# Attention values in four 32-column tiles, softmax sums as separate products, roots on ScalarE, in a planned GNN kernel

## Chip, cores and metric

One core of a Trainium2 chip. The metric is device microseconds of one execution. The profile is of one execution of the same program.

## The reference, cut to what matters

The kernel computes two layers on 16 graphs of 1024 nodes with 256 features. The first layer is masked attention with 8 heads of 32 columns:

```python
e = jnp.einsum('whqd,whkd->whqk', q, k)
e = jnp.where(e >= 0, e, ALPHA * e)
attn = jax.nn.softmax(jnp.where(adj[:, None] > 0, e, NEG), axis=-1)
h = jnp.einsum('whqk,whkd->whqd', attn, v)
out = _layernorm(h.transpose(0, 2, 1, 3).reshape(w, n, H * DH), g1, b1)
out = jnp.concatenate([out, features], axis=-1) @ Wffn.T
x = _layernorm(out, g2, b2) + features
```

The second layer applies two graph attentions (scores are a sum of a row term and a column term, softmax over the masked graph, then a product with the node rows), adds the residual, normalizes, and runs a feed-forward net of 256 to 1024 to 256 columns with a second residual and normalization. All is float32.

## The kernel before

The work of one graph is called a batch; `b` counts them. A head's 1024 x 1024 scores are made transposed, keys on partitions, in 8 tiles `t` of 128 keys by 1024 queries. Each tile goes through a chain of four engines:

- `all_scores` (L601): TensorE, two matmuls of 512 columns into a PSUM tile `ps_s` (two such tiles).
- `weights`: ScalarE multiplies by 0.2 (L619), VectorE takes the larger of that and the score (L621), ScalarE takes the exponential (L624), GpSimd multiplies by the mask (L628). The result is `p`, one of 5 buffers.
- `all_values` (L650): TensorE multiplies by `v`. The 33 columns of a head are 32 values and one column of -1, so that row 33 of the result is the softmax sum. The two halves of the queries go to rows 0 and 64 of one PSUM bank `ps_a`, as two column tiles of the array.
- `after_head`: the bank is copied out (`ho`), transposed (L677), and the values are divided by the sum (L682, L684).

The products of values are issued in pairs of tiles:

```python
for t in range(d, d + GV):
    p = probs.pop((b, h, t))
    for nh in range(NH):
        m = VW if t else 64
        nc.tensor.matmul(acc[nh * 64:nh * 64 + m, :], v[:, t, c:c + m],
                         p[:, nh * HALF:(nh + 1) * HALF], start=(t == 0), stop=(t == NT - 1))
```

`project` makes the transposed features, queries, keys and values of the next batch (L475, L507), and `make_mask` turns its adjacency into 8-bit masks (L412, L422). `rest` does all that follows the attention of the batch before: `rows_pair`, the two graph attentions (`attend` on VectorE, L838 and L841; products L876 and L901), `normed_pair`, and the feed-forward net (L941, L969). So TensorE always has work of two batches at hand. `stats` computes a normalization's mean and variance on VectorE, and the reciprocal root on GpSimd as an addition (L338) and a power (L340).

The order of instructions on every engine is written by a planner at build time. `Order` runs each function above as a thread. A thread announces an operation with its cost (`on`), waits for events, takes and gives buffers, and has an aim, a due time that is a share of a batch's length `SLOT` (the tables `AIM` and `EARLY`). The planner keeps a clock for each engine, adds a hand-over time `HOP` between engines, treats the operations marked `shared` on VectorE and GpSimd as exclusive, and among the operations that could begin within `WINDOW` ns emits the one due first. The chip then runs each engine's list in that order; the waits between engines are semaphores that the framework adds. DMAs are issued from SP (`qk_halves`, `qs`, `ks`, `x_kept`, the outputs) and from ScalarE (`adj_i`, `xr`).

PSUM buffers for all other products (`ps_m`, taken with `misc`) are a ring of three.

Of the kernel before, what the change touches and what calls it, by code (L numbers as in the profile page):

```python
# [18 lines left out]
EPS = 1e-5  # L19
H = 8  # L20
P = 128
# [13 lines left out]
class Order:  # L35
# [5 lines left out]

    HOP = dict(PE=100.0, ACT=70.0, DVE=60.0, POOL=70.0, SP=60.0)
    WINDOW = 300.0

# [3 lines left out]
    def __init__(self, **pools):  # L54
        self.clock = defaultdict(float)
        self.port = 0.0
        self.transfers = 0.0
        self.stretch, self.done, self.half = 0, 0.0, True
        self.pools = {k: [0.0] * n for k, n in pools.items()}
        self.queues = defaultdict(list)  # L60
        self.events = {}
        self.waiting = defaultdict(list)
        self.active = []
        self.made = 0
        self.now = 0.0
        self.busy = defaultdict(float)

    def add(self, thread, aim, ready=0.0):
        self.made += 1
        self.step({"gen": thread, "aim": aim, "no": self.made, "ready": ready}, None)  # L70

    def step(self, th, sent):
        while True:
# [19 lines left out]
            elif what == "take":  # L93
# [3 lines left out]
                th["ready"] = max(th["ready"], self.pools[arg].pop(0))  # L97
            elif what == "give":
                queue = self.queues[arg]
                if queue:  # L100
                    other = min(queue, key=lambda o: (o["aim"], o["no"]))
                    queue.remove(other)
                    other["ready"] = max(other["ready"], th["ready"])
                    self.step(other, None)
                else:
                    self.pools[arg].append(th["ready"])
                    self.pools[arg].sort()
# [26 lines left out]
    def run(self):  # L134
        while self.active:
            could = []
            for th in self.active:
                costs, shared, delay = th["op"]
                best = None
                for engine, cost in costs.items():  # L140
                    ready = th["ready"]
                    if th.get("last", ())[:2] == (engine, ready):
                        ready -= self.HOP[engine]
                    t = max(self.clock[engine], ready)
                    if shared and engine in ("DVE", "POOL"):
                        t = max(t, self.port)
                    if best is None or t + cost < best[0] + best[2]:
                        best = t, engine, cost
                could.append((best, th))
            first = min(c[0][0] for c in could)  # L150
            (t, engine, cost), th = min((c for c in could if c[0][0] <= first + self.WINDOW),
                                        key=lambda c: (c[1]["aim"], c[1]["no"]))
            if th["op"][1] and engine in ("DVE", "POOL"):

                lead = 100.0 if engine == "DVE" else -100.0
                before = [c for c in could if c[1]["op"][1] and c[0][1] in ("DVE", "POOL")
                          and c[0][1] != engine and c[0][0] + lead < t]
                if before:
                    (t, engine, cost), th = min(before, key=lambda c: (c[1]["aim"], c[1]["no"]))
            costs, shared, delay = th["op"]  # L160
            self.active.remove(th)
            end = self.clock[engine] = self.end(engine, t, cost)
# [4 lines left out]
            th["ready"] = end + self.HOP[engine]  # L167
# [10 lines left out]
def on(shared=False, delay=0.0, **costs):  # L178
    return "on", (costs, shared, delay)
# [45 lines left out]
def unshifted_path(  # L225
# [19 lines left out]
    VW = DH + 1  # L245
    GV = 2
    YW = D + 2
# [6 lines left out]
    AIM = dict(mask0=0.759, x=0.818, x_step=0, mask=0.747, mask_step=0.0264, qk0=0.614, qk1=0.898,  # L254
               qk_step=0.0231, v0=0.832, v1=0.974, v_step=0.0591, rows=-0.244, rows_step=0.0408, first0=0.12,
               first1=0.252, graph0=-0.009, graph1=0.21, graph_step=0, second=0.355, second_step=0.0335,
               normed=0.78, normed_step=0.026, ff_wait=(None, 0, 1, 0), ff=(0.532, -0.011, 0.487, 0.497),
               ff_step=0.0386, fast0=0.425, fast1=0.938, fast15=0.832, lead=3.15)

    EARLY = dict(x=0.87, x_step=0.005, mask=0.747, mask_step=0.0296, qk0=0.692, qk1=0.909, qk_step=0.0345,  # L260
                 v0=0.774, v1=1.001, v_step=0.0568, rows=-0.139, rows_step=0.0071, first0=0.082, first1=-0.169,
                 graph0=-0.195, graph1=-0.027, graph_step=0, second=0.302, second_step=0.0335, normed=0.781,
                 normed_step=0.02, ff_wait=(None, 0, 1, 0), ff=(0.633, -0.001, 0.488, 0.497), ff_step=0.0386)
# [6 lines left out]
    bufs = dict(misc=3, scores=2, acc=1, p=5, stacks=2, stage=2, adj=2, adjb=2, pair=18,  # L270
# [6 lines left out]
    def misc(dtype=FT):  # L277
        return psum.tile([P, HALF], dtype, tag="misc", name="ps_m", bufs=bufs["misc"])
# [9 lines left out]
    minus_half = const.tile([P, TPH], FT, name="minus_half")  # L288
    nc.gpsimd.memset(minus_half, -0.5)
# [25 lines left out]
    def evacuate(n):  # L315
        return on(DVE=140 + 1.06 * n, ACT=150 + 0.87 * n)

    def evacuate_by(n):

        return on(DVE=190 + 1.06 * n, ACT=250 + 0.87 * n)  # L320
# [5 lines left out]
    def stats(srcs):  # L326
# [3 lines left out]
        for i, src in enumerate(srcs):  # L330
            st = small.tile([P, 6], FT, name="st")
            yield on(DVE=420)
            nc.vector.bn_stats(st, src)
            yield on(DVE=185)
            nc.vector.bn_aggr(mv[:, i, :], st)  # L335
        rs = small.tile([P, n], FT, name=f"rs{n}")
        yield on(POOL=260)
        nc.gpsimd.tensor_scalar(rs, mv[:, :, 1], EPS, None, op0=OP.add)  # L338
        yield on(POOL=450 + 150 * n, shared=True)
        nc.gpsimd.tensor_tensor(rs, rs, minus_half[:, :n], op=OP.pow)  # L340
        return mv, rs

    def normalized(dst, srcs, mv, rs):
        for i, (row, src) in enumerate(zip(dst, srcs)):
            if row is src:
                yield on(DVE=340, shared=True)
            else:
                yield on(DVE=440)
# [38 lines left out]
    def mask_part(b, t, halves):  # L387
# [22 lines left out]
        for i, ai in enumerate(ints):  # L410
            yield on(DVE=440, shared=True)
# [8 lines left out]
        yield on(PE=90 + 112 * n)  # L420
# [3 lines left out]
        yield on(ACT=150 + 225 * n)  # L424
# [19 lines left out]
    def x_pair(b, u):  # L444
# [7 lines left out]
        yield on(PE=450)  # L452
# [7 lines left out]
    def qk_part(b, g, o, nh):  # L460
# [12 lines left out]
        yield on(PE=1720)  # L473
# [3 lines left out]
        yield on(ACT=590)  # L477
        nc.scalar.copy(high.bitcast(FR), pa)
        yield on(DVE=690)
# [20 lines left out]
    def v_part(b, g, u):  # L500
# [3 lines left out]
        yield on(PE=1000)  # L504
# [6 lines left out]
        dst = vs[b, g][:, 2 * u:2 * u + 2, :G * VW].rearrange("p t (h c) -> p t h c", c=VW)[:, :, :, :DH]  # L511
        src = pa[:, :2 * P].rearrange("p (t h c) -> p t h c", t=2, c=DH)
# [7 lines left out]
    def project_v(b, g, t0):  # L520
        yield take("v")
        v = buf([P, NT, G * VW + 31], "v", "v")
        vs[b, g] = v
        yield on(POOL=500)
        nc.gpsimd.memset(v[:, :, G * VW:], 0.0)
        nc.gpsimd.memset(v[:, :, :G * VW].rearrange("p t (h c) -> p t h c", c=VW)[:, :, :, DH:], -1.0)
# [3 lines left out]
    def warm_up():  # L530
# [3 lines left out]
        nc.scalar.copy(small.tile([P, TPH], FT, name="warm", bufs=1), minus_half)  # L534
# [46 lines left out]
    def all_scores():  # L581
        for b in range(B):
# [4 lines left out]
            for h in range(H):  # L587
                yield wait(("stack", b, h))
                q, kk = stacks[b, h]
                n = 2 if b else 1  # L590
                for t in range(0, NT, n):
                    due = t0 + (h * NT + t) / 2 * pace(b)
                    yield aim(due, AIM["lead"] * PACE)
                    for _ in range(n):
                        yield take("scores")
                    ps = [psum.tile([P, N], FT, tag="scores", name="ps_s") for _ in range(n)]
                    yield on(PE=450 * n)
                    for i in range(n):
                        for nh in range(NH):
                            cols = slice(nh * HALF, (nh + 1) * HALF)  # L600
                            nc.tensor.matmul(ps[i][:, cols], kk[:, (t + i) * P:(t + i + 1) * P], q[:, cols],  # L601
                                             start=True, stop=True)
                    if t + n == NT:
                        yield give("stacks")
                    for i in range(n):
                        yield start(weights(b, h, t + i, ps[i]), due + i * PACE / 2)

    def weights(b, h, t, ps):
# [3 lines left out]
        if b == 0:  # L612
            engine = yield on(ACT=1050, DVE=1230)
        else:
            engine = yield on(ACT=1050)
# [4 lines left out]
        yield on(DVE=1220)  # L620
        nc.vector.tensor_tensor(p, p, ps, op=OP.max)  # L621
        yield give("scores")
        yield on(ACT=1080)
# [3 lines left out]
        yield on(POOL=2050, shared=True)  # L627
# [3 lines left out]
    def all_values():  # L631
        for b in range(B):
            for h in range(H):
                g, c = h // G, (h % G) * VW
# [4 lines left out]
                acc = psum.tile([P, HALF], FT, tag="acc", name="ps_a", bufs=bufs["acc"])  # L639
                for d in range(0, NT, GV):  # L640
                    for t in range(d, d + GV):
                        yield wait(("p", b, h, t))
                    yield aim(begin[b] + (h * NT + d + 2) / 2 * pace(b), SLOT)
                    yield on(PE=240 + 860 * GV)
                    for t in range(d, d + GV):
                        p = probs.pop((b, h, t))
                        for nh in range(NH):

                            m = VW if t else 64
                            nc.tensor.matmul(acc[nh * 64:nh * 64 + m, :], v[:, t, c:c + m],  # L650
                                             p[:, nh * HALF:(nh + 1) * HALF],
                                             start=(t == 0), stop=(t == NT - 1))
                    for t in range(GV):
                        yield give("p")
                yield start(after_head(b, h, acc), begin[b] + (h + 1) * NT // 2 * pace(b))
                if h % G == G - 1:
                    yield give("v")
            yield start(rest(b), work.now)

    def after_head(b, h, acc):  # L660
# [6 lines left out]
        used = 64 + VW  # L667
# [7 lines left out]
        yield on(PE=450)  # L675
        for i in range(TPH):
            nc.tensor.transpose(pt[:, i * P:i * P + used], ho[:used, i * P:(i + 1) * P], ident[:used, :used])  # L677
        yield give("pair")
        src = pt.rearrange("p (i j c) -> p j i c", i=TPH, j=NH)
# [766 lines left out]
```

## Time and profile before

| What | Value |
|---|---|
| Runs shown, median of 3 | 4487.69 us (4481.99 to 4490.15) |
| Profiled execution, first to last instruction | 4479.9 us |
| TensorE matmuls, busy | 4325.9 us, 20299 records |
| TensorE weight loads, busy | 2866.3 us |
| VectorE busy | 3311.9 us |
| ScalarE busy | 2887.7 us |
| GpSimd busy | 2474.9 us |
| Mean granted TensorE clock | 0.990 |

Of the profiled execution the page gives the span alone, so its time is the span; the median of the runs is 7.8 us above it, 0.2%. A record of a matmul has a modelled end, so its mean duration holds the time that its results take to come out; how long it keeps the array is seen from the distance of two starts. A float32 matmul leaves two records. An engine's idle time is put down to what ended it, not to what was slow.

### The profile page before, as it was taken

Reading aid. Unit: us, or ns where it says so; the run is one execution under the profiler, and the core shown is the slowest. Engines: PE = TensorE matmul, PEld = TensorE weight load, DVE = VectorE, ACT = ScalarE, POOL = GpSimd, SP = SyncE. Lnnn points to the kernel's source line nnn. Section 1 sums busy time; section 2 is a strip of 40 time slices with the busy share of each in tenths; the row PEclk is TensorE's granted clock in tenths of the full one; section 3 lists DMA queues with packets and bytes.
Section 4 is the critical chain, followed back from the end, with each engine's and each line's share of the span. In section 5 each row is a group of like instructions: output and inputs, shape, how many; then the busy total and the mean of one; then the engine's idle time right before and its main releaser. Section 6 shows DMA issues by size and latency. Waiting matters only on the chain.

```text
span 4479.9 us, 57088 instructions
## 1 busy us (share of the span) xinstructions
PE 4325.9 (97%) x20299; PEld 2866.3 (64%) x20299; DVE 3311.9 (74%) x5263; ACT 2887.7 (64%) x4015; POOL 2474.9 (55%) x1544
## 2 busy tenths in 40 slices
PE   8888999999999999999999999999999999999998
PEld 3444656667666675766667666676666667666587
DVE  6877867687776877778777776877778777776754
ACT  6666675666667666666666666666666666666631
POOL 5756565554565556556554565546556554665610
PEclk9989999999999999999999999999999999999999
DMA  6423222232232313223231232323223231232100
GB/s 187 114 66 87 66 73 77 73 92 73 68 88 63 107 59 86 76 59 99 64 106 55 74 96 62 103 63 80 80 64 99 64 102 55 71 92 55 27 22 20
DMA packets 156209, 343.57 MB, mean 77 GB/s; under 512 B 21751, under 2 KB 24333, under 8 KB 155917
## 3 DMA queue, kind: packets, MB, share of 16 engines
q1 hardware_dynamic: 112140, 260.13, 20.8%
q10 hardware_dynamic: 43776, 79.71, 6.1%
q8 instruction: 164, 2.69, 0.3%
q14 instruction: 129, 1.05, 0.1%
HBM read 239.09 MB, written 100.66 MB: 76 GB/s over the span
## 4 chain that ended last, share of the span: by engine, by line
PE 69%; DVE 18%; issue 5%; POOL 5%; ACT 2%; DMA 0%; POOLq 0%; ACTq 0%; DVEq 0%
PE ps_a L650 16%; PE ps_s L601 9%; PE ps_m L901 8%; PE ps_m L876 8%; PE ps_m L941 7%; PE ps_m L969 6%; DVE att L841 5%; DVE att L838 5%; POOL p L628 4%; DVE p L621 4%; PE ps_m L785 3%; PE ps_m L475 3%; PE ps_m L753 2%; PE ps_m L756 2%; PE ps_m L355 2%
## 5 line engine op out<-in xcount | busy, mean ns | idle before, releaser
L628 POOL TENSOR_TENSOR p<-p,mask 128x1024 f32<-128x1024 f32 x1024 | 2232.2, 2197 | 1564.6 <-ACT p L624 1444.7
L621 DVE TENSOR_TENSOR p<-p,ps_s 128x1024 f32<-128x1024 f32 x1024 | 1211.1, 1214 | 399.3 <-ACT p L619 397.8
L624 ACT ACTIVATE p<-p 128x1024 f32<-128x1024 f32 x1024 | 1080.9, 1058 | 377.5 <-DVE p L621 355.7
L619 ACT ACTIVATE p<-ps_s 128x1024 f32<-128x1024 f32 x995 | 974.9, 1025 | 186.7 <-PE ps_s L601 172.1
L650 PE MATMUL ps_a<-p,v 128*33 128x512 f32 (+1 forms) x4096 | 1000.6, 606 | 24.2 <-POOL p L628 22.9
L601 PE MATMUL ps_s<-qs,ks 128*128 128x512 f32 x2048 | 634.5, 428 | 39.2 <-DVE p L621 38.3
L601 PEld LDWEIGHTS ps_s<-qs,ks 128*128 128x128 f32 x2048 | 349.5, 190 | 343.2 <-DVE p L621 106.2
L650 PEld LDWEIGHTS ps_a<-p,v 128*33 128x33 f32 (+1 forms) x4096 | 199.7, 114 | 531.3 <-issue 405.3
L901 PE MATMUL ps_m<-y,att 128*128 128x256 f32 x2048 | 480.5, 380 | 12.7 <-ACT v L516 11.0
L941 PE MATMUL ps_m<-rT,wf 128*128 128x256 f32 x2048 | 479.8, 384 | 10.7 <-ACT z L313 3.6
L969 PE MATMUL ps_m<-wf,hid 128*128 128x256 f32 x2048 | 475.1, 381 | 10.6 <-ACT xT L313 8.9
L876 PE MATMUL ps_m<-y,att 128*128 128x258 f32 x2048 | 472.4, 381 | 0.0
L969 PEld LDWEIGHTS ps_m<-wf,hid 128*128 128x128 f32 x2048 | 379.4, 190 | 78.6 <-issue 14.8
L876 PEld LDWEIGHTS ps_m<-y,att 128*128 128x128 f32 x2048 | 385.2, 189 | 63.6 <-issue 3.3
L901 PEld LDWEIGHTS ps_m<-y,att 128*128 128x128 f32 x2048 | 375.0, 189 | 77.3 <-ACT v L516 13.1
L941 PEld LDWEIGHTS ps_m<-rT,wf 128*128 128x128 f32 x2048 | 380.9, 192 | 63.4 <-ACT z L313 3.8
L838 DVE SCALAR_TENSOR_TENSOR att<-first,second 128x1024 f32<-128x1024 f32 x256 | 354.4, 1384 | 73.2 <-ACT first L825 73.2
L841 DVE SCALAR_TENSOR_TENSOR att<-mask,att 128x1024 f32<-128x1024 fp8e4 x256 | 352.0, 1375 | 8.7
L846 ACT ACTIVATE y<-y,check 128x258 f32<-128x258 f32 x256 | 130.9, 511 | 305.3 <-DVE check L844 278.4
L338 POOL TENSOR_SCALAR rs<-mv 128x2 f32<-128x2 f32 (+1 forms) x224 | 60.0, 268 | 410.9 <-DVE mv L335 410.8
L412 DVE TENSOR_SCALAR adj_b<-adj_i 128x512 fp8e4<-128x512 int32 x256 | 234.0, 958 | 14.8 <-DMA adj_i<-in_adj_dram 9.3
L950 ACT ACTIVATE hid<-ps_m,columns 128x256 f32<-128x256 f32 x372 | 159.2, 472 | 119.8 <-PE ps_m L941 94.3
(105 smaller groups left out, 4232.5 us busy)
## 6 DMA issues: line engine op xcount, KB each, us to landing
qs<-qk_halves SPq DMA_DIRECT2D x256, 256.0 KB, 4.2
ks<-qk_halves SPq DMA_DIRECT2D x256, 256.0 KB, 5.1
adj_i<-in_adj_dram ACTq DMA_DIRECT2D x240, 256.0 KB, 3.5
qk_halves<-high SPq DMA_DIRECT2D x128, 256.0 KB, 2.4
qk_halves<-low SPq DMA_DIRECT2D x128, 256.0 KB, 3.6
xr<-in_x_dram ACTq DMA_DIRECT2D x64, 256.0 KB, 3.1
x_kept<-x SPq DMA_DIRECT2D x64, 256.0 KB, 4.8
x<-x_kept SPq DMA_DIRECT2D x64, 256.0 KB, 6.8
```

Source lines behind the costliest of these rows:

```text
L601: nc.tensor.matmul(ps[i][:, cols], kk[:, (t + i) * P:(t + i + 1) * P], q[:, cols], start=True, stop=True)
L619: nc.scalar.activation(p, ps, AF.Copy, scale=ALPHA)
L621: nc.vector.tensor_tensor(p, p, ps, op=OP.max)
L624: nc.scalar.activation(p, p, AF.Exp)
L628: nc.gpsimd.tensor_tensor(p, p, mask_of(b, t), op=OP.mult)
L650: nc.tensor.matmul(acc[nh * 64:nh * 64 + m, :], v[:, t, c:c + m], p[:, nh * HALF:(nh + 1) * HALF], start=(t == 0), stop=(t == NT - 1))
L838: nc.vector.scalar_tensor_tensor(e, first[:, 0, :], second[:, j:j + 1], first[:, 1, :], op0=OP.mult, op1=OP.max)
L841: nc.vector.scalar_tensor_tensor(e, mask_of(b, j), -1.0, e, op0=OP.mult, op1=OP.mult, accum_out=sums[:, j:j + 1])
L876: nc.tensor.matmul(pa[:, cols:cols + width], big[:, j, i * P:(i + 1) * P], rows[:, j, :width], start=(j == 0), stop=(j == NT - 1))
L901: nc.tensor.matmul(pa[:, i * D:(i + 1) * D], big[:, j, t * P:(t + 1) * P], y2[:, j, :D], start=(j == 0), stop=False)
L941: nc.tensor.matmul(pa[:, i * 2 * P:(i + 1) * 2 * P], wf1[:, dc, hc * P:(hc + 1) * P], rT[:, dc, :], start=(dc == 0), stop=(dc == DC - 1))
L969: nc.tensor.matmul(pa[:, i * D:(i + 1) * D], hid[hc // 2][:, hc % 2, i * P:(i + 1) * P], wf2[:, hc, :], start=(hc == 0), stop=False)
```

## The change

- `v` has no columns of -1. A tile's values are four matmuls of 32 columns by 256 queries, each to its own 32 rows of the bank's first half. The sums are four matmuls of the same shape with a constant block of -1 as weights, to the bank's second half.
- Of a head's four pairs of tiles, the first two are added on VectorE (`add_pair`), and the sum product is taken of the added tile, behind the values of the next pair. The last two pairs have a sum product for each tile. `p` has 6 buffers.
- The transposes of `after_head` cover all 128 rows.
- `stats` takes the root on ScalarE: a logarithm, then an exponential of -0.5 times it. The activation table is loaded by name at the start.
- Scores are planned one tile at a time in every batch.
- The planner has new costs for most operations, a hand-over before (`HOP`) and after (`TAIL`) an operation, a cost `SWITCH` for TensorE's change between tiled and whole-array products, another rule for the order of `shared` operations, and new due times. The three `ps_m` buffers have a tag each, and a product takes the one that the planner chose.

```diff
-    HOP = dict(PE=100.0, ACT=70.0, DVE=60.0, POOL=70.0, SP=60.0)
+    HOP = dict(PE=53.0, ACT=35.0, DVE=36.0, POOL=80.0, SP=60.0)
+    TAIL = dict(PE=163.0, ACT=103.0, DVE=84.0, POOL=42.0, SP=0.0)
     WINDOW = 300.0
+    SWITCH = 93.0
...
-                lead = 100.0 if engine == "DVE" else -100.0
                 before = [c for c in could if c[1]["op"][1] and c[0][1] in ("DVE", "POOL")
-                          and c[0][1] != engine and c[0][0] + lead < t]
+                          and c[0][1] != engine and c[0][3] < asked]
...
+            if engine == "PE":
+                if narrow != self.narrow:
+                    cost += self.SWITCH
+                self.narrow = narrow
...
-    bufs = dict(misc=3, scores=2, acc=1, p=5, stacks=2, stage=2, adj=2, adjb=2, pair=18,
+    bufs = dict(misc=3, scores=2, acc=1, p=6, stacks=2, stage=2, adj=2, adjb=2, pair=18,
...
-        return psum.tile([P, HALF], dtype, tag="misc", name="ps_m", bufs=bufs["misc"])
+        return psum.tile([P, HALF], dtype, tag=f"misc{work.slot['misc']}", name="ps_m", bufs=1)
...
+    minus_ones = const.tile([P, DH], FT, name="minus_ones")
+    nc.gpsimd.memset(minus_ones, -1.0)
...
         rs = small.tile([P, n], FT, name=f"rs{n}")
-        yield on(POOL=260)
-        nc.gpsimd.tensor_scalar(rs, mv[:, :, 1], EPS, None, op0=OP.add)
-        yield on(POOL=450 + 150 * n, shared=True)
-        nc.gpsimd.tensor_tensor(rs, rs, minus_half[:, :n], op=OP.pow)
+        yield on(ACT=98)
+        nc.scalar.activation(rs, mv[:, :, 1], AF.Ln, bias=eps)
+        yield on(ACT=98)
+        nc.scalar.activation(rs, rs, AF.Exp, scale=-0.5)
...
-        v = buf([P, NT, G * VW + 31], "v", "v")
-        vs[b, g] = v
-        yield on(POOL=500)
-        nc.gpsimd.memset(v[:, :, G * VW:], 0.0)
-        nc.gpsimd.memset(v[:, :, :G * VW].rearrange("p t (h c) -> p t h c", c=VW)[:, :, :, DH:], -1.0)
+        vs[b, g] = buf([P, NT, G * DH], "v", "v")
...
-                n = 2 if b else 1
-                for t in range(0, NT, n):
+                for t in range(NT):
...
+                def product(w, p, at, first, last):
+                    for i in range(4):
+                        nc.tensor.matmul(acc[i * DH:(i + 1) * DH, at:at + QN], w, p[:, i * QN:(i + 1) * QN],
+                                         start=first, stop=last)
+
+                added = []
                 for d in range(0, NT, GV):
+                    last, adds = d + GV == NT, d < ADDED * GV
                     for t in range(d, d + GV):
                         yield wait(("p", b, h, t))
+                    if added:
+                        yield wait(("p added", b, h, d - GV))
                     yield aim(begin[b] + (h * NT + d + 2) / 2 * pace(b), SLOT)
-                    yield on(PE=240 + 860 * GV)
...
+                    ps = [probs.pop((b, h, t)) for t in range(d, d + GV)]
+                    for t, p in zip(range(d, d + GV), ps):
+                        yield on(PE=430, narrow=True)
+                        product(v[:, t, c:c + DH], p, 0, t == 0, False)
+                        yield aim(begin[b], BIG)
+                    if adds:
+                        yield start(add_pair(b, h, d, ps), begin[b] + (h * NT + d + 2) / 2 * pace(b))
+                    for p in added if adds else added + ps:
+                        yield on(PE=430, narrow=True)
+                        product(minus_ones, p, QN, False, last and p is ps[-1])
                         yield give("p")
+                    added = ps[:1] if adds else []
...
+    def add_pair(b, h, d, ps):
+        yield on(DVE=1180, shared=True)
+        nc.vector.tensor_tensor(ps[0], ps[0], ps[1], op=OP.add)
+        yield give("p")
+        yield fire(("p added", b, h, d))
...
-            nc.tensor.transpose(pt[:, i * P:i * P + used], ho[:used, i * P:(i + 1) * P], ident[:used, :used])
+            nc.tensor.transpose(pt[:, i * P:(i + 1) * P], ho[:, i * P:(i + 1) * P], ident)
```

Nearly every other `on(...)` has a new cost in the same manner, and every entry of `AIM` and `EARLY` that the batches use is changed.

## Prediction

> **What bounds the kernel now.** I read the busy table first, then the groups of instructions, then the timeline of one stretch of TensorE, then the table of stages, and last the waits of the weight loads.
>
> ```profile
> PE 4325.9 (97%) x20299; PEld 2866.3 (64%) x20299; DVE 3311.9 (74%) x5263; ACT 2887.7 (64%) x4015; POOL 2474.9 (55%) x1544
> ```
>
> TensorE is busy for 97% of the span, the next engine (VectorE) for 74%. A busy PE is not yet a PE at its peak, so the groups and the timeline must show what its time is made of.
>
> ```profile
> L628 POOL TENSOR_TENSOR p<-p,mask 128x1024 f32<-128x1024 f32 x1024 | 2232.2, 2197 | 1564.6 <-ACT p L624 1444.7 <-issue 72.6 <-PE ps_m L941 11.7
> L621 DVE TENSOR_TENSOR p<-p,ps_s 128x1024 f32<-128x1024 f32 x1024 | 1211.1, 1214 | 399.3 <-ACT p L619 397.8
> L650 PE MATMUL ps_a<-p,v 128*33 128x512 f32 (+1 forms) x4096 | 1000.6, 606 | 24.2 <-POOL p L628 22.9
> L412 DVE TENSOR_SCALAR adj_b<-adj_i 128x512 fp8e4<-128x512 int32 x256 | 234.0, 958 | 14.8 <-DMA adj_i<-in_adj_dram 9.3 <-PE ps_m L422 5.4
> L340 POOL TENSOR_TENSOR rs<-rs,minus_half 128x2 f32<-128x2 f32 (+1 forms) x224 | 177.0, 790 | 18.3
> L677 PE MATMUL ps_m<-ident,ho 97*128 97x97 f32 x512 | 66.8, 253 | 14.2 <-ACT ho L313 8.6 <-DVE ho L311 3.5 <-DVE rT L372 1.2
> L338 POOL TENSOR_SCALAR rs<-mv 128x2 f32<-128x2 f32 (+1 forms) x224 | 60.0, 268 | 410.9 <-DVE mv L335 410.8
> L859 ACT ACTIVATE second<-check 128x8 f32<-128x8 f32 x2 | 0.4, 201 | 0.0
> ```
>
> The value product (L650) is the costliest work of the busiest engine: 1000.6 us, 22% of the span. Its 4096 records are two per f32 matmul. The last line is of one batch's window; it prices a tiny Exp.
>
> ```profile
> 2039.01 3.62 PE L901 MATMUL ps_m<-y,att 128*128 128x256 f32 x16
> 2042.56 1.91 PE L650 MATMUL ps_a<-p,v 128*33 128x512 f32 x8
> 2044.40 1.20 PE L601 MATMUL ps_s<-qs,ks 128*128 128x512 f32 x4
> 2052.29 1.88 PE L475 MATMUL ps_m<-xT,wq 128*128 128x512 f32 x4
> 2054.01 0.39 PE L422 MATMUL ps_m<-ident_b,adj_b 128*128 128x128 bf16 x4
> ```
>
> Read the starts, not the modelled durations. Four records of 512 columns on the whole array (L475) last from 2052.29 to 2054.01, 0.43 us each. Eight such records of L650 last from 2042.56 to 2044.40, 1.84 us: four slots of 0.43 are 1.72, so two column tiles run side by side at full rate, and 0.09 is left over at each end (L901: 16 records of 0.216 are 3.45, L650 starts after 3.55). The single records agree: the two tiles start 7 ns apart, pairs follow every 429 ns, and entering or leaving the tiled mode adds 93 ns.
>
> I priced every matmul record of the trace so, at its smallest steady distance to the next: streaming 4019 us (L650 873 of it), 1024 mode switches 95 us, real idle 352 us. **TensorE is the bound, with 8% of slack.** The slack lies here:
>
> ```profile
> 0.00:140.00 140.00, 116.97 (x474) 53.12 (x476) 104.61 (x115) 86.84 (x117) 86.55 (x54) 0.93 0.61 179
> 140.00:280.00 140.00, 120.88 (x546) 65.66 (x543) 111.57 (x160) 90.60 (x128) 93.42 (x53) 0.90 0.30 85
> 2000.00:2270.00 270.00, 266.16 (x1265) 177.65 (x1264) 203.95 (x326) 182.25 (x254) 152.72 (x96) 1.00 0.28 79
> ```
>
> Columns after the width: PE, PEld, DVE, ACT, POOL busy, clock, DMA share, GB/s. Batch 0 has too little other work beside its softmax chain: 132 of the 352 us idle fall in the first 560 us. From then on a batch lasts 270 us, the sum of 259 us of streaming and switches and 11 us idle. In those steady batches the waits of the weight loads are short:
>
> ```profile
> PEld ps_a L650 <- POOL p L628: 56.2, 89, 1.7
> PEld ps_s L601 <- DVE p L621: 55.1, 65, 2.7
> ```
>
> (560 to 4060 us; us, times, longest.) Less TensorE work therefore shortens the program, as long as the chain ACT, DVE, ACT, POOL of each score tile keeps up.
>
> **What the Trainium skill says.** "TensorEngine Tiling (Array Packing)", Key Properties: tiles run independently, and changing the tiling mode drains the engine. The trace agrees: 7 ns between two tiles, 93 ns per switch. "TensorE: Matmul & The Clock Gate", Measured speedup vs the span model: four row tiles gave 3.07 times, three column tiles 2.38 times. The trace has two column tiles only, at 2.0 times (429 ns per pair against 429 for one); four are not shown. "SBUF — State Buffer", Who interferes with whom: VectorE and GpSimd share a port pair under an exclusive lock. The trace agrees: L412 takes 409 ns at best, 958 on average, 2379 at worst. "ScalarE: Activation LUTs", Table sets: Exp and Ln lie in one set. Before has a single table load; the instruction streams show one in the changed kernel too.
>
> **The change part by part.**
>
> *Value products.* Each of 1024 score tiles is now multiplied by 32 columns of v in four tiles of 256 columns: 4096 matmuls, where before 2048 went in two tiles of 512. The sums have their own products with a block of -1: pairs 0 and 1 of a head's four are added first, so six products a head and not eight, 768 in all, 3072 matmuls. Together 7168 matmuls, two records each. A 256-column record takes 216 ns (L901 above); four abreast, 7168 x 2 x 0.216 / 4 = 774 us. Before: 873. **-99 us.** Bounds: with perfect overlap 774; at the skill's 3.07 times 1009 (+136). I take 4.0, since two tiles measure exactly 2.0 in a stream, while a single burst also pays the pipeline's fill; weight loads of the next slot start within 30 ns for two tiles and take 110 ns, so four fit under 216.
>
> *Switches.* In the changed instruction stream the tiled products form 515 runs, where before there were 512. The cost stays at 96 us (+0.6).
>
> *Head transposes.* L677 goes from 97 to 128 columns: 512 records, 83 ns apart now, 109 like other 128-column transposes: **+13 us.**
>
> TensorE's sum: -99 + 1 + 13 = **-85 us**; pricing the two instruction streams record by record, with the same prices, gives 4149 and 4056, **-92**. I use -90. A steady batch goes from 259 to 253 us of work.
>
> *Pair additions.* 256 additions of 128x1024 on VectorE, priced at L621's 1.21 us: +310 us. Both inputs lie in SBUF, so the port lock counts: at most another 0.54 each as L412 waits on average, 449 in all. Evictions that the plan moves between VectorE and ScalarE (81 fewer of hid, 30 more of v, 23 more of hT and rT, 13 of xT) give about -20. VectorE comes to 3600 us, 82% of the new span; in a steady batch 204 + 19 = 223 of 264. I cost it at nothing, covered by TensorE's queue of other products; without that cover it is up to 1.2 us a pair. An addition must wait for both value products of its pair and stands in VectorE's queue ahead of later max operations (L621), for which score products wait. It also keeps a p buffer until the next pair's product; a sixth p buffer is added for it.
>
> *Roots.* 448 POOL instructions (60 + 177 us) go, and 32 pairs of memsets (15); ScalarE gets 448 of some 0.2 us, +90. POOL falls to about 2223, ScalarE rises to about 3000 (69%). A root no longer stands behind a 2.2 us mask product, but behind 1 us exponentials. VectorE's 58 us of idle ahead of L349 shrink. Worth on the path: 0 to -15 us.
>
> *Re-planning.* New costs, aims, scores one tile at a time, and PSUM slots that follow the plan's choice instead of a ring. DMAs keep their numbers (1001 on SP); their order against other work moves. Distance of a score product's end from its value product, in TensorE work of a steady batch: smallest 8.0 before, 6.8 after; median 9.7 and 12.3. The chain needs 1.03 + 1.21 + 1.06 + 2.14 = 5.4 us and its hand-overs, so it still fits, with less room at the low end. Idle outside L650 and L601 is 162 us; slot order can touch only that. Bounds for all idle: -120 (a third less) to +60 (5 us more a batch, half again). I take -15, the roots alone.
>
> *Sum.* 4479.9 - 90 - 15 = 4375 for the span. The median of the runs shown is 7.8 above the profiled span, so **4382 us**, 2.4% less.
>
> **The rivals.**
> 1. *The plan gains more than the products.* Idle in the head shrinks from 132 to 70 and a steady batch's from 11 to 7: another -100, 4285 us. For it: 162 us idle at buffers. Against it: batch 0 gets more VectorE work, where VectorE is at 75 to 80% already.
> 2. *VectorE takes the place of the bound.* Port waits double each addition, and L621 comes late: 16 x 1.2 x 16 batches = 307 us more in VectorE's queue, of which a fifth to a third reaches TensorE, +60 to +100: 4440 to 4485 us, hardly a gain. For it: 85% busy in a steady batch. The share is my choice. Against it: half of the value products lie 12 us or more of TensorE work behind their scores.
> 3. *Slower: four tiles don't run four abreast* (place L645, price 3097 us / c for the tiled products). 3097 / c - 873 + 14 is zero at c = 3.6; below that the change loses. At c = 3.07 it is +150: 4638 us. Against it: exact doubling with two.
>
> **How the numbers follow.** Likeliest case 0.60 (4335 to 4425); rival 1 0.20; rival 2 0.12, a third of it no better than before; rival 3 0.08. About 0.2% (9 us) is what a measurement of this kernel can tell from no change. Faster 0.86, same 0.04, slower 0.10. The range, 4275 to 4455, leaves out rival 3, the worse part of rival 2, and the end of rival 1.
>
> **What would show it.** In the changed profile: four records of the value product within 30 ns, slots 216 ns apart, together about 774 us of streaming; PE's busy time down by 80 to 110; additions near 1.2 us (over 1.6: port waits); a steady batch near 264 us; a single table load. Wrong: slots of 250 ns or more (rival 3), or waits of the weight loads on L621 and L628 well above 111 us in the steady part (rival 2).

## The result, and the profile after

The changed kernel takes 4433.2 us (median of 4 runs, 4430.1 to 4435.8) against 4486.0 us before (4 runs as well): a ratio of 0.9882 (95% interval 0.9869 to 0.9895). That is 53 us, 1.2%, where 104 us were forecast. The table of busy time and the costliest groups of the changed kernel:

```profile
PE 4267.4 (96%) x30539; PEld 3082.5 (70%) x30539; DVE 3515.0 (79%) x5493; ACT 3004.8 (68%) x4488; POOL 2364.4 (53%) x1033
```
```profile
L630 POOL TENSOR_TENSOR p<-p,mask 128x1024 f32<-128x1024 f32 x1024 | 2363.6, 2332 | 1837.8 <-ACT p L626 1338.2 <-ACT mask L437 316.4 <-PE ps_a L645 94.3
L645 PE MATMUL ps_a<-p,v 128*32 128x256 f32 x8192 | 559.2, 388 | 12.2 <-POOL p L630 12.2
L645 PE MATMUL ps_a<-p,minus_ones 128*32 128x256 f32 x6144 | 407.9, 383 | 31.8 <-DVE p L675 31.5
L675 DVE TENSOR_TENSOR p<-p 128x1024 f32<-128x1024 f32 x256 | 374.1, 1461 | 18.2 <-PE ps_a L645 16.8
```

TensorE is still the bound. The span is 46 us shorter (4433.9), TensorE's busy time 58 us. GpSimd lost 237 us of roots, but its busy time fell by 110 only: the mean mask product grew from 2197 to 2332 ns. A piece of TensorE's timeline:

```profile
2040.91 1.07 PE L645 MATMUL ps_a<-p,v 128*32 128x256 f32 x16
2041.79 0.61 PE L645 MATMUL ps_a<-p,minus_ones 128*32 128x256 f32 x8
2042.34 0.73 PE L605 MATMUL ps_s<-qs,ks 128*128 128x512 f32 x2
2042.91 0.38 PE L947 MATMUL ps_m<-ident,x 128*128 128x128 f32 x2
```

The starts say that four tiles do run four abreast: 16 records take 0.88 us, four slots of 0.216. In the single records the four start within 21 ns and the next four follow 196 ns later. What is new stands in the third line: a lone score tile keeps TensorE for 0.57 us, while the pair of before took 1.03, 0.52 each.

The same stages as before (width, then PE, PEld, DVE, ACT, POOL busy), and the two waits of the weight loads from 560 to 4060 us:

```profile
0.00:140.00 140.00, 113.50 (x804) 60.66 (x808) 97.03 (x107) 91.16 (x122) 89.14 (x47) 0.94 0.57 169
140.00:280.00 140.00, 111.14 (x841) 69.31 (x833) 112.73 (x168) 85.86 (x134) 78.39 (x33) 0.94 0.36 101
2000.00:2270.00 270.00, 266.38 (x1949) 193.27 (x1949) 219.81 (x342) 191.79 (x286) 149.38 (x66) 1.00 0.29 82
```
```profile
PEld ps_s L605 <- DVE p L623: 55.8, 102, 2.2
PEld ps_a L645 <- POOL p L630: 19.2, 42, 0.8
```

TensorE is busy for less of the first 280 us than before (225 us, before 238): there the work that was taken away turned into idle time. A steady batch lasts 266.8 us, where it lasted 270.1. Waits for masks fell (19 us, before 56), those for VectorE's maximum came more often (102 times, before 65).

One kind of wait is new. The three longest waits of a matmul, 9.5, 9.4 and 9.5 us at 285, 394 and 4171 us, are of a sum product for its addition. First the total of such waits, then the first of the three on TensorE and on VectorE, and the stretch around it:

```profile
PE ps_a L645 <- DVE p L675: 31.5, 5, 9.5
```
```profile
285.44 1.08 PE L645 MATMUL ps_a<-p,minus_ones 128*32 128x256 f32 x8 [9.48 <-DVE p L675]
288.79 3.64 PE L894 MATMUL ps_m<-y,att 128*128 128x258 f32 x8
292.36 1.52 PE L645 MATMUL ps_a<-p,v 128*32 128x256 f32 x16
```
```profile
281.52 1.26 DVE L856 SCALAR_TENSOR_TENSOR att<-first,second 128x1024 f32<-128x1024 f32 x1
282.82 1.22 DVE L859 SCALAR_TENSOR_TENSOR att<-mask,att 128x1024 f32<-128x1024 fp8e4 x1
284.17 1.22 DVE L675 TENSOR_TENSOR p<-p 128x1024 f32<-128x1024 f32 x1
```
```profile
279.70:293.30 13.60, 6.61 (x30) 3.87 (x34) 11.37 (x15) 7.15 (x9) 3.29 (x2) 0.50 0.17 58
```

VectorE doesn't stand still here: it works through a graph attention (L856, L859), and the addition stands behind that in its list. The granted clock is 0.50 meanwhile. Eight records of L894 last 3.57 us there (288.79 to 292.36); at full clock, 0.217 us each, they would take 1.74. Before, no matmul waited longer than 4.4 us.

I priced the records of every trace as in the prediction, with the slot distances of two and four tiles measured separately (hence 346 where the prediction has 352). Streaming is what the records take at these prices, switches is the change between tiled and whole-array products, and idle is the rest. A record counts for no more than the distance to the next one, so kernels with the same matmuls differ by up to 17 us in streaming. The three columns are of the profiled execution; with 13 to 14 us before its first matmul and behind its last they make its span, while the time is the median of the runs:

| Kernel | Time | Streaming | Switches | Idle |
|---|---|---|---|---|
| before | 4486 | 4025 | 95 | 346 |
| after | 4433 | 3921 | 96 | 404 |
| additions of 8 columns | 4404 | 3921 | 96 | 372 |
| after, no additions, re-planned | 4559 | 4026 | 99 | 419 |
| after, old products, re-planned | 4534 | 4008 | 94 | 417 |
| before, four tiles, no additions, order kept | 4461 | 3932 | 95 | 419 |
| before, two planner costs changed | 4731 | 4018 | 95 | 601 |
| after, due times fitted anew, ring | 4396 | 3924 | 99 | 357 |

Streaming fell by 104 us; idle rose by 58. The idle column also holds what a lower clock costs. The traces show stretches of 3.4 us, or a multiple of it, with half the clock granted, mostly at a wait of TensorE or right behind it, and 256-column records follow there every 427 ns instead of 215. (The planner reckons with such stretches, by its `STRETCH` and `WORK`.) Matmuls were busy for 75 us of these stretches before and for 59 after. Half of that is lost, about 37 and 30 us by this estimate, so the clock doesn't explain the 58. The experiments ask where these 58 came from.

### The profile page after: what moved, and what is told of

Its sections match the earlier page's. It is cut to its first block, busy times and chain, and to the rows that moved or that the text cites. A ratio compares the mean times of both kernels' runs of the same rounds, so it can differ in the third digit from the quotient of the medians.

```text
span 4433.9 us, 77232 instructions
## 1 busy us (share of the span) xinstructions
PE 4267.4 (96%) x30539; PEld 3082.5 (70%) x30539; DVE 3515.0 (79%) x5493; ACT 3004.8 (68%) x4488; POOL 2364.4 (53%) x1033
## 4 chain that ended last, share of the span: by engine, by line
PE 67%; DVE 28%; ACT 3%; issue 2%; POOL 0%; DMA 0%; ACTq 0%; SPq 0%; DVEq 0%; POOLq 0%
PE ps_a L645 15%; PE ps_s L605 10%; PE ps_m L894 9%; PE ps_m L919 8%; DVE att L856 7%; DVE att L859 6%; DVE p L623 5%; PE ps_m L959 4%; PE ps_m L486 4%; PE ps_m L987 3%; PE ps_m L771 3%; PE ps_m L803 2%; PE ps_m L774 2%; ACT p L621 2%; PE ps_m L366 1%
## 5 line engine op out<-in xcount | busy, mean ns | idle before, releaser
L630 POOL TENSOR_TENSOR p<-p,mask 128x1024 f32<-128x1024 f32 x1024 | 2363.6, 2332 | 1837.8 <-ACT p L626 1338.2
L621 ACT ACTIVATE p<-ps_s 128x1024 f32<-128x1024 f32 x1006 | 996.0, 1020 | 198.2 <-PE ps_s L605 91.9
L605 PE MATMUL ps_s<-qs,ks 128*128 128x512 f32 x2048 | 684.7, 439 | 50.6 <-DVE p L623 46.6
L645 PE MATMUL ps_a<-p,v 128*32 128x256 f32 x8192 | 559.2, 388 | 12.2 <-POOL p L630 12.2
L605 PEld LDWEIGHTS ps_s<-qs,ks 128*128 128x128 f32 x2048 | 337.1, 190 | 276.2 <-issue 116.5
L894 PE MATMUL ps_m<-y,att 128*128 128x258 f32 x2048 | 484.6, 382 | 5.5 <-ACT y L864 1.9
L894 PEld LDWEIGHTS ps_m<-y,att 128*128 128x128 f32 x2048 | 386.4, 190 | 76.7 <-ACT hid L968 6.1
L645 PE MATMUL ps_a<-p,minus_ones 128*32 128x256 f32 x6144 | 407.9, 383 | 31.8 <-DVE p L675 31.5
L645 PEld LDWEIGHTS ps_a<-p,v 128*32 128x32 f32 x8192 | 213.4, 109 | 288.7 <-issue 155.2
L675 DVE TENSOR_TENSOR p<-p 128x1024 f32<-128x1024 f32 x256 | 374.1, 1461 | 18.2 <-PE ps_a L645 16.8
L856 DVE SCALAR_TENSOR_TENSOR att<-first,second 128x1024 f32<-128x1024 f32 x256 | 370.1, 1446 | 13.5 <-ACT first L843 13.5
L859 DVE SCALAR_TENSOR_TENSOR att<-mask,att 128x1024 f32<-128x1024 fp8e4 x256 | 343.8, 1343 | 7.7
L645 PEld LDWEIGHTS ps_a<-p,minus_ones 128*32 128x32 f32 x6144 | 199.0, 111 | 172.4 <-DVE p L675 41.3
```

The costliest lines, as they stand in the source:

```text
L605: nc.tensor.matmul(ps[:, cols], kk[:, t * P:(t + 1) * P], q[:, cols], start=True, stop=True)
L621: nc.scalar.activation(p, ps, AF.Copy, scale=ALPHA)
L630: nc.gpsimd.tensor_tensor(p, p, mask_of(b, t), op=OP.mult)
L645: nc.tensor.matmul(acc[i * DH:(i + 1) * DH, at:at + QN], w, p[:, i * QN:(i + 1) * QN], start=first, stop=last)
L856: nc.vector.scalar_tensor_tensor(e, first[:, 0, :], second[:, j:j + 1], first[:, 1, :], op0=OP.mult, op1=OP.max)
L859: nc.vector.scalar_tensor_tensor(e, mask_of(b, j), -1.0, e, op0=OP.mult, op1=OP.mult, accum_out=sums[:, j:j + 1])
```

## Experiments

The theories at the start were: A, the additions' time on VectorE; B, the new plan; C, the roots on ScalarE. D, due times that fit one order only, came after the first four runs. The runs were timed in four groups, each with the kernel before beside it on the same chip; each ratio is to before in its own group.

### Additions cut short (order kept)

```diff
-        nc.vector.tensor_tensor(ps[0], ps[0], ps[1], op=OP.add)
+        nc.vector.tensor_tensor(ps[0][:, :8], ps[0][:, :8], ps[1][:, :8], op=OP.add)
```

> The changed kernel with each pair addition cut to 8 of its 1024 columns, so most of the second tile is left out of the softmax sums; every engine's list of instructions stays the same. Theory A (the additions' time on VectorE, some 374 us, delays the score chain and gave back 58 us of TensorE idle time): idle falls from 404 us to about 345 or below, time 4345 to 4385 us. Rival B (the new plan's order leaves the idle, additions or not): within 10 us of 4433. Rival C (roots on ScalarE delay it): the same as B.

Measured: 4404.0 us, ratio 0.9821 (0.9804 to 0.9837). That is 29 us below the changed kernel, idle 372: about half of A's forecast. The groups of this kernel:

```profile
L675 DVE TENSOR_TENSOR p<-p 128x8 f32<-128x8 f32 x256 | 127.1, 496 | 38.5 <-PE ps_a L645 37.8
L630 POOL TENSOR_TENSOR p<-p,mask 128x1024 f32<-128x1024 f32 x1024 | 2233.3, 2202 | 1935.7 <-ACT p L626 1437.0 <-ACT mask L437 326.5 <-PE ps_a L645 99.1
```

The mask products are back at 2202 ns, so their extra 130 ns came with the additions' length. That agrees with the exclusive lock of the Trainium skill's "SBUF — State Buffer", Who interferes with whom, in both directions: an addition of 8 columns still takes 496 ns in the mean (133 at best, 160 in the median, 2018 at worst). So 29 us is the price of the additions' length. Their places in VectorE's list and their port waits remain in this kernel, and with them the three long waits of a sum product (8.4, 7.7 and 8.4 us):

```profile
PE ps_a L645 <- DVE p L675: 26.1, 4, 8.4
```

### No additions, re-planned

```diff
-    ADDED = 2
+    ADDED = 0
```

> The changed kernel with ADDED = 0: eight sum products per head, no additions, re-planned. The planned lists price 115 us more of tiled products and mode switches. Theory A: idle falls by about 55 us, so 4490 to 4505 us, slower than before the change. Rival B: idle stays at 404, about 4548 us.

Measured: 4559.1 us, ratio 1.0165 (1.0148 to 1.0182), idle 419. Nearer to B's number than to A's. But this kernel has another order as well, which the next runs show to matter.

### Old products under the new plan

The tiled products, sums and additions are taken out of the changed kernel:

```diff
-                        yield on(PE=430, narrow=True)
-                        product(v[:, t, c:c + DH], p, 0, t == 0, False)
...
+                    yield on(PE=860 * GV, narrow=True)
+                    for t in range(d, d + GV):
```

> The changed kernel with the value products of before (two tiles of 33 columns, sums in the 33rd, 5 p buffers) under the new plan, PSUM slots, single score tiles and roots on ScalarE. TensorE's work is that of before. Theory A: the plan is neutral, 4475 to 4495 us, idle about 346. Rival B: the plan itself leaves 40 us or more of idle, 4525 us or above. If the plan is what won: below 4460.

Measured: 4533.9 us, ratio 1.0108 (1.0091 to 1.0125), idle 417. The new plan without the new products is 48 us slower than before.

### Roots on ScalarE in the kernel before: re-planned, and with the order kept

```diff
-        yield on(POOL=260)
-        nc.gpsimd.tensor_scalar(rs, mv[:, :, 1], EPS, None, op0=OP.add)
-        yield on(POOL=450 + 150 * n, shared=True)
-        nc.gpsimd.tensor_tensor(rs, rs, minus_half[:, :n], op=OP.pow)
+        yield on(ACT=200)
+        nc.scalar.activation(rs, mv[:, :, 1], AF.Ln, bias=eps)
+        yield on(ACT=200)
+        nc.scalar.activation(rs, rs, AF.Exp, scale=-0.5)
```

> The kernel before with the roots alone moved to ScalarE (logarithm and exponential), re-planned with the old aims. Theory A says nothing of roots: within 15 us of 4486. My prediction's step: 0 to 15 us faster. Rival C (roots delay ScalarE's chain): slower by 20 us or more.

Measured: 4711.7 us, ratio 1.0506 (1.0488 to 1.0523). C seemed to win by far. The control leaves the two `on(POOL=...)` lines in place and changes the operations alone:

> The kernel before with its order of all other instructions kept: the planner still books the roots on GpSimd, but a logarithm and an exponential on ScalarE are issued in their place. Rival C (the roots themselves delay ScalarE's chain): 4600 us or more, as with the re-planned roots (4712). Theory D (a plan whose due times were fitted to other work loses 50 to 230 us; the roots themselves cost or gain little): 4470 to 4500 us.

Measured: 4490.6 us, ratio 1.0011 (1.0004 to 1.0018). The roots cost 5 us in this order; the other 221 us came with the new order.

### A re-plan and nothing else

```diff
-        yield on(POOL=260)
+        yield on(POOL=268)
-        yield on(POOL=450 + 150 * n, shared=True)
+        yield on(POOL=650 + 70 * n, shared=True)
```

> The kernel before, its planner's two costs for a root set to the durations that the trace shows (268 and 790 ns for two rows, instead of 260 and 750); the operations are the same, the order is planned anew. Theory D (the due times fit one order only): slower by 40 us or more. Rival (a re-plan is harmless, and the 226 us were the roots'): within 20 us of 4486.

Measured: 4730.8 us, ratio 1.0548 (1.0530 to 1.0565). That is 245 us longer. The two costs were no better than the old ones. The 790 ns of the expectation are a mean over roots of two and of four rows, and the parts of the kernel before are:

```profile
L340 POOL TENSOR_TENSOR rs<-rs,minus_half 128x2 f32<-128x2 f32 x192 | 143.8, 749 | 15.7
L340 POOL TENSOR_TENSOR rs<-rs,minus_half 128x4 f32<-128x4 f32 x32 | 33.1, 1036 | 2.6
```

The old costs, 750 and 1050, fit them; the new ones are 790 and 930. The test holds all the same: two costs moved by 3 to 11%, and the order with them. Busy time of this kernel and the longest of its weight loads' waits for another engine's work, in total:

```profile
PE 4400.4 (93%) x20299; PEld 2904.9 (61%) x20299; DVE 3446.6 (73%) x5409; ACT 2833.2 (60%) x3869; POOL 2518.4 (53%) x1544
```
```profile
PEld ps_s L601 <- DVE p L621: 175.2, 155, 9.8
```

The work is the same, but the plan also chose VectorE for 146 evictions (reads of a result out of PSUM) that ScalarE had done (5409 and 3869 instructions, before 5263 and 4015). Score products wait for VectorE's maximum for 175 us in place of 106, once for 9.8 us, and all idle rises from 346 to 601. Some 48 us of this rise are the clock's, by the estimate above: matmuls were busy for 171 us of half-clock stretches, before for 75. So a part that is taken out with a re-plan is measured together with the loss of a fitted order. Theory D holds here, and the three re-planned runs above price no part of the change.

### Roots back on GpSimd in the changed kernel (order kept)

```diff
         yield on(ACT=98)
-        nc.scalar.activation(rs, mv[:, :, 1], AF.Ln, bias=eps)
+        nc.gpsimd.tensor_scalar(rs, mv[:, :, 1], EPS, None, op0=OP.add)
         yield on(ACT=98)
-        nc.scalar.activation(rs, rs, AF.Exp, scale=-0.5)
+        nc.gpsimd.tensor_tensor(rs, rs, minus_half[:, :n], op=OP.pow)
```

> The changed kernel with its order kept, the roots issued to GpSimd as before, in ScalarE's place. My prediction's step (roots on ScalarE are worth 0 to 15 us): 4433 to 4448 us. If the roots on ScalarE delay the chain: below 4425. If GpSimd's port lock and queue matter more than I said: above 4450.

Measured: 4462.4 us, ratio 0.9955 (0.9938 to 0.9971), 29 us above the changed kernel. The roots of this kernel, then those of the changed one:

```profile
L351 POOL TENSOR_TENSOR rs<-rs,minus_half 128x2 f32<-128x2 f32 (+1 forms) x224 | 189.7, 847 | 18.6
L360 DVE TENSOR_SCALAR y<-y,mv,rs 128x256 f32<-128x256 f32 x256 | 187.2, 766 | 47.3 <-POOL rs L351 46.9
```
```profile
L351 ACT ACTIVATE rs<-rs 128x2 f32<-128x2 f32 (+1 forms) x224 | 45.7, 204 | 6.8
L360 DVE TENSOR_SCALAR y<-y,mv,rs 128x256 f32<-128x256 f32 x256 | 170.5, 701 | 13.1 <-ACT rs L351 12.4
```

VectorE stands idle ahead of the normalization for 47 us with roots on GpSimd, 13 with them on ScalarE. In the order of before the move didn't shorten this wait. First the kernel before, then the one with its order kept and roots on ScalarE:

```profile
L349 DVE TENSOR_SCALAR y<-y,mv,rs 128x256 f32<-128x256 f32 x256 | 137.4, 570 | 46.6 <-POOL rs L340 45.6
```
```profile
L349 DVE TENSOR_SCALAR y<-y,mv,rs 128x256 f32<-128x256 f32 x256 | 156.9, 646 | 49.7 <-ACT rs L340 48.6
```

So ScalarE alone doesn't make the root early; the place that the new plan gives it was not tested by itself. The order was made for roots on ScalarE, so 29 us is what their loss costs there. How much of it goes through the normalization is not shown: with roots on GpSimd, that engine also waits 1082 us for variances, with mask products behind it, and additions take 1567 ns in place of 1461.

### Products of the change in the order of before

Additions right after their pair's products, outside the plan, into a buffer of their own:

```diff
+                    if adds:
+                        added = [sb.tile([P, N], FT, tag="added", name="added", bufs=1)]
+                        nc.vector.tensor_tensor(added[0], ps[0], ps[1], op=OP.add)
```

> The kernel before with its order kept and only the value products changed: four 32-column tiles, separate sums, two pairs of four added on VectorE into a buffer of their own right after the pair's products (5 p buffers and that one). TensorE's work falls by about 93 us (tiled products 106 less, transposes 13 more). Theory A (additions give back some 30 us, the rest is gain): 4415 to 4435 us. Rival B (work taken from TensorE without a new plan turns into idle time): 4460 us or above.

Measured: 5011.0 us, ratio 1.1173 (1.1154 to 1.1192). The number is in B's open range, but idle time that only takes back a saving can't make the kernel 525 us slower than before. The addition's group and its wait:

```profile
L661 DVE TENSOR_TENSOR added<-p 128x1024 f32<-128x1024 f32 x256 | 438.3, 1712 | 219.4 <-PE ps_a L651 213.8 <-POOL p L628 2.5 <-issue 1.0
```
```profile
DVE added L661 <- PE ps_a L651: 213.8, 122, 4.2
```

An addition waits up to 4.2 us for the sum product that still reads the one buffer, and the maxima behind it in VectorE's list wait too. The buffer and the place are not told apart by this run. So the same without additions:

```diff
+                    for p in ps[:1] if adds else ps:
+                        product(minus_ones, p, QN, False, last and p is ps[-1])
```

> The kernel before with its order kept, the value products as four 32-column tiles with six separate sum products a head, and no additions: the second tile of each of the first two pairs is left out of the softmax sums. TensorE's work falls by about 93 us and VectorE gets nothing more. Theory A' (the saving of TensorE's work turns into time where nothing is added to VectorE): 4385 to 4405 us. Rival B (under an order fitted to more work, half or more of the saving turns into idle time): 4435 us or above.

Measured: 4460.7 us, ratio 0.9947 (0.9931 to 0.9964). Streaming is 93 us less, as priced, but idle is 73 more, and only 24 us come through. That is rival B without the additions: in an order fitted to more work, most of the saving turns into waits. Whether a new order for these products would give it back was not run. Against this kernel the additions of the run above cost 550 us, 2 us each. Some 145 us of these are the clock's by the estimate above, for matmuls were busy for 380 us of half-clock stretches there and for 89 here.

### The slots of ps_m

```diff
-        return psum.tile([P, HALF], dtype, tag=f"misc{work.slot['misc']}", name="ps_m", bufs=1)
+        return psum.tile([P, HALF], dtype, tag="misc", name="ps_m", bufs=bufs["misc"])
```

> The changed kernel with its order kept and the three ps_m buffers a ring again, as before, in place of the slots that the planner chose. If the slots are worth nothing: within 10 us of 4433. If they carry part of the gain (a ring makes products wait for a buffer while another is free): 20 us or more above it.

Measured: 4423.9 us, ratio 0.9864 (0.9848 to 0.9881). The ring is 9 us ahead in the medians, but the intervals of the two ratios overlap: the slots bring nothing that these runs can show.

### Due times fitted anew

All entries of `AIM` and `EARLY` were searched further for the earliest end of the planner's own clock (which is no time of the chip), with the ring:

```diff
-               first1=0.2264, graph0=0.0576, graph1=0.273, graph_step=0.0015, second=0.3518, second_step=0.0609,
...
+               first0=0.1153, first1=0.3227, graph0=0.0667, graph1=-1.5443, graph_step=0.008,
...
-               ff_step=0.0581, fast0=0.4431, fast1=0.9245, fast15=0.6119, lead=1.5024)
...
+               fast15=0.6493, lead=9.9515)
```

> The changed kernel with a ring for the ps_m buffers and other due times (AIM, EARLY), fitted longer to the same operations; nothing else differs. Theory D (what the change left idle is in the order, which can be fitted further): 10 to 40 us below the ring's 4424, at 4384 to 4414 us. Rival (the idle is in VectorE's added time, whatever the order): within 10 us of 4424.

Measured: 4396.4 us, ratio 0.9811 (0.9795 to 0.9828): faster than both kernels. Its busy time:

```profile
PE 4244.4 (97%) x30539; PEld 3087.4 (70%) x30539; DVE 3488.7 (79%) x5486; ACT 3012.9 (69%) x4495; POOL 2352.9 (54%) x1033
```

> As the run before, with a second, independently fitted set of due times that the planner holds for a little worse. Theory D: 4390 to 4420 us, so that two different orders both gain. Rival: within 10 us of 4424 or above.

Measured: 4421.0 us, ratio 0.9869 (0.9853 to 0.9886), no better than the ring alone. One of two new orders gained, so D's forecast holds for the first only. What the first gained is idle time: 357 us, with streaming as it was and additions of 1494 ns. The ring's kernel still has the three long waits for an addition (9.5, 9.0 and 9.5 us). The first set of due times has none of them; in place of the first two stand waits of 13.8 and 12.2 us for ScalarE, in place of the third none. The second set keeps two (9.5 and 9.4 us).

## Why the prediction was half right

The direction and the range held (4275 to 4455); the forecast of 4382 was 51 us too fast. The measured 4433 lies outside the likeliest case (4335 to 4425), between it and rival 2 (4440 to 4485), so the range held by its width. By its own steps:

- **Products, -99: right.** Tiled products went from 878 to 772 us, -106. The four tiles run at 4.0 times one in a stream, as two run at 2.0. The 3.07 times for four row tiles of the Trainium skill's "TensorE: Matmul & The Clock Gate" (Measured speedup vs the span model) doesn't describe a stream like this one; the measurement decides. Rival 3 is out.
- **Switches, +1: right** (515 runs; 96 us). The wider transposes show 10 of their 13 us (41 to 51). TensorE's sum is -103 against the -90 used. Some 10 us of the difference are only booked elsewhere, as the idle step says.
- **Additions at nothing: wrong.** They take 1.46 us in the mean and not 1.21, they make mask products 0.13 us longer, and their length costs 29 us of the span. Rival 2 named the mechanism; its share (a fifth to a third of the added time) was 29 of 374 us for the length, while the price of their places in the list is not measured. Its sign, waits of the weight loads on L621 and L628 well above 111 us in the steady part, did not appear: the same two waits came to 75 us.
- **Roots, 0 to -15: missed on both sides.** In the order of before the move cost 5 us; in the order of the changed kernel it is worth 29. A price that holds without the order was not found.
- **Idle, -15: this is the step that failed.** It rose by 58. Its bounds were -120 to +60, and I took the roots alone, as if the re-plan gave back what the thinner cover takes. The additions' length is 29 of them. Some 22 can be counted in the trace: a score tile that follows anything but a score tile mostly holds its first matmul for 316 to 337 ns, where it is 234 behind a score tile. Before, with pairs, 518 tiles started so; after, with single tiles, 667, and the time above the price of 229 ns goes from 59 to 81 us. About half of the 22 is bookkeeping: the record ahead of such a start is often followed after 28 ns, whatever its own price, and counts that much less as streaming (23 us less before, 34 after). The net is 11 us. I listed single tiles under the re-plan and gave them no price. No run isolates this count.
- **Where it lies:** 21 of the 58 in the first 280 us, some 40 between 560 and 4060 us, and next to nothing from 280 to 560 us, where two of the long waits stand in place of others. Batch 0 has no other work to put under its chain, so its 174 us are 7 more than before although it has less for TensorE. I predicted for the whole span that less TensorE work shortens the program; it holds for the steady batches, which went from 259 to 253 us of work and from 270.1 to 266.8 us of time. Rival 1 saw idle shrink there and in the head; it grew in both.

What stays open is how much of the rise is the order's own: the count of 22 is not isolated, the long waits for an addition stay when the additions are short, and how the rest divides is not shown. The fitted orders show only that an order with 47 us less idle exists for the same operations.

## What to carry to other kernels

Price a saving on the bound engine as work and as cover: what it no longer does, it no longer hides, and in an in-order plan fitted to the old work three quarters of it can come back as waits (24 of 93 us got through here). Test a part of a planned kernel with the order kept, since a re-plan with two costs changed by 3 to 11% moved this one by 5.5%. And ask of each instruction put into an in-order queue what stands behind it: the length of 256 additions cost 29 us where they were planned, and the additions cost 550 (5011 against 4461) where they were not and had one buffer.

## What the runs showed of the hardware

- Four column tiles of 32 in float32 start within 21 ns and follow each other every 216 ns: a full factor of four.
- The first matmul of a score tile behind other work mostly held the array for 316 to 337 ns instead of 234 (about 420 behind records of 256 columns). In the single records of a typical one, the second weight load starts 108 ns after the first and the second matmul 336 ns after the first; 336 less 229 is 107, so by this estimate the first load was not hidden.
- A VectorE addition of 8 columns of two SBUF tensors took 496 ns in the mean beside GpSimd's 2.2 us products, and 160 in the median.
- The granted clock was halved in stretches of 3.4 us or a multiple, mostly at a wait of TensorE or right behind it: 17 stretches and 91 us in the kernel before, 38 and 233 us in the one with two planner costs changed. In them 256-column records followed every 427 ns instead of 215.
